# A planned order of instructions, and VectorE operations that use both SBUF ports kept apart from GpSimd in the plan

## Chip, cores, metric

The kernel runs on one core of one Trainium2 chip. Its time is device microseconds (us) of one execution; what is given is the median of several. VectorE is DVE in the profile, ScalarE is ACT, GpSimd is POOL, TensorE is PE (its weight loads PEld), SyncE is SP.

## What is computed

Two sequences of 1024 tokens, 288 features, run through four layers one after the other. Layers L0 and L1 are quantised transformer blocks: self-attention (16 heads of 18), cross-attention to 154 context tokens with a mask, and a feed-forward part of 1152. L2 and L3 are plain cross-attentions with two softmaxes, one over 86 and one over 68 context tokens, whose outputs are added.

```python
def quant_act(x):
    s = max(abs(x), axis=-1) / 127 + 1e-8
    q = clip(round(x / s), -127, 127)
    return q, s, sum(q, axis=-1)
def quant_linear(q, s, qsum, w, b):      # w quantised row by row, with a zero point zw
    acc = q @ qw.T - qsum * zw
    return acc * (s * sw) + b
# L0, L1
h = layer_norm(x, g1, b1); x = x + lin(attn(lin(h), lin(h), lin(h)))
h = layer_norm(x, g2, b2); x = x + lin(attn(lin(h), cond @ wk2.T, cond @ wv2.T, mask))
h = layer_norm(x, g3, b3); x = x + lin(gelu(lin(h)))
# L2, L3
x = x + sdpa(q, k, v) @ Wo.T + sdpa(q, k_vip, v_vip) @ Wo_vip.T
```

Every `lin` of L0 and L1 on the tokens is a `quant_act` followed by a `quant_linear`.

## The kernel before

The tokens stay in SBUF as `x`, 16 chunks of 128 tokens. Self-attention takes a head group of four heads and 512 queries at a time, in two sweeps: one finds the maximum of each row of logits (PE L1000 into PSUM, then DVE `tensor_reduce` L1007), the other computes the logits again with the maximum taken off, the exponential (PE L1060, ACT L1062) and the weighted sum of the values (PE L1074, four matmuls of 32 columns side by side, called strips). Cross-attention of L0 and L1 copies the logits out of PSUM (ACT L1040), adds the mask on GpSimd (L1041) and reduces them from SBUF (DVE L1046); its second sweep adds the mask on DVE (L1146). L2 and L3 reduce from PSUM.

Beside these sweeps run the side chains: layer norms, quantisations, weights.

- `ln_quantise`: DVE statistics (L809, L810), the power on GpSimd (L814), scale and shift on ACT (L822), gain and bias on GpSimd (L830, two `tensor_tensor` of 128x288 for each chunk), then `quantise`.
- `quantise`: DVE maximum (L773), scale (L774), reciprocal (L775), GpSimd parts (L780 to L783), DVE multiply and round (L785, `tensor_scalar` in SBUF), ACT (L789), DVE sums (L799, L800).
- `quantise_rows` for weights: small DVE operations (L627 to L637), two `tensor_scalar` for each third (L640, L643), then GpSimd (L648, L653 to L661, and `three`, L613 to L616).
- `split` and `add_to_x` put `tensor_tensor` on GpSimd (L910, L917, L872). `Features.add` (L1210) scales the outputs of L2 and L3 on DVE.

The program text gives only the dependencies. The order on each engine comes from the kernel's own planner at build time: `Plan` reads all instructions, `duration` gives each a latency and a time for which it holds its engine, `forward` is a list scheduler over the five queues (it keeps, for each engine, the ready instructions by rank and starts the best of them when the engine is free), and `backward` makes the ranks. `arrange` runs `forward` with ranks from `backward` 16 times, keeps the plan whose modelled end is the earliest, and chains the instructions of each engine in that order with dependencies that carry no semaphore:

```python
    for line in orders.values():
        for one, other in zip(line, line[1:]):
            order_behind(tc, insts[other], insts[one])
```

So the plan fixes the sequence on each engine, and nothing of the planned times. On the chip an instruction starts when its engine has reached it and its semaphores allow it. In the plan before, DVE and GpSimd know nothing of each other but data.

Of the kernel before, what the change touches and what calls it, by code (L numbers as in the profile page):

```python
# [113 lines left out]
    return t, t - 42  # L114


def region(arg):

    ap = arg.bass_ap
    tensor, dims, at = ap.tensor, list(ap.ap), ap.offset  # L120
    p0, p1 = 0, 1
    if tensor.space != bass.MemoryType.DRAM:
        row = math.prod(tensor.shape[1:])
        p0, at = divmod(at, row)
        step, count = dims.pop(0)
        p1 = p0 + (count - 1) * max(step // row, 0) + 1
    bits = 1
    for step, count in dims:
        if step and count > 1:
            one, made, left = bits, 1, count  # L130
            bits, shift = 0, 0
            while left:
                if left & 1:
                    bits |= one << shift
                    shift += step * made
                left >>= 1
                if left:
                    one |= one << (step * made)
                    made *= 2
    return tensor, p0, p1, bits << at  # L140


class Plan:


    def __init__(self, insts, ties):
        self.insts, n = insts, len(insts)
        self.after = [{} for _ in insts]
        self.need = [0] * n
        self.engine = [None] * n  # L150
        self.times = [(0.0, 0.0)] * n
        self.claims = [[] for _ in insts]
        self.ends = [[] for _ in insts]
        self.bufs, self.turn, self.tag_of = {}, {}, {}
        self.group, self.strip, self.table = {}, [False] * n, [None] * n
        touched, tiles, opened, closed, lead = {}, {}, {}, None, None
        for at, inst in enumerate(insts):
            k, kind = at, type(inst).__name__
            if kind == "BassTilePoolBoundary":
                if inst.op == "release":  # L160
                    closed = k
                    for t in inst.bass_pool_tiles or ():
                        for j in tiles.get(t.name, ()):
                            self.edge(j, k)
                elif closed is not None:
                    opened[inst.bass_pool_name] = closed
                continue
            if not kind.startswith("Inst") or not len(inst.outs):
                continue
            if kind == "InstMatmult" and inst.tile_size[1] == 32:  # L170
                if lead is None or len(self.group[lead]) == 4:
                    lead, self.group[at] = at, []
                k = lead
                self.group[k].append(at)
                self.strip[k] = True
            if kind == "InstActivation" and inst.func != AF.Identity:
                self.table[k] = inst.func
            self.engine[k] = inst.engine.name
            if k == at:
                self.times[k] = duration(inst) if kind != "InstRegisterMove" else (60.0, 60.0)  # L180
            uses = [(a, False) for a in inst.ins] + [(a, True) for a in inst.outs]
            for arg, writes in uses:
                if not hasattr(arg, "bass_ap"):
                    continue
                tensor = arg.bass_ap.tensor
                name, in_dram = tensor.name, tensor.space == bass.MemoryType.DRAM
                if hasattr(tensor, "tag"):
                    if name not in tiles and not in_dram:
                        self.claim(k, tensor)
                        pool = tensor.tag.rsplit("_", 2)[-2]  # L190
                        if pool in opened:
                            self.edge(opened[pool], k)
                    users = tiles.setdefault(name, [])
                    for j in users[:1]:
                        self.edge(j, k, False) if j != k else None
                    users.append(k)
                elif in_dram:
                    continue
                _, p0, p1, bits = region(arg)
                log, kept = touched.setdefault(name, []), []  # L200
                for j, wrote, q0, q1, c in log:
                    if (writes or wrote) and j != k:
                        if p0 < q1 and q0 < p1 and bits & c:
                            self.edge(j, k)
                        elif self.engine[j] == self.engine[k] and wrote and writes:
                            self.edge(j, k, False)
                    if not (writes and p0 <= q0 and q1 <= p1 and j != k and not c & ~bits):
                        kept.append((j, wrote, q0, q1, c))
                kept.append((k, writes, p0, p1, bits))
                touched[name] = kept  # L210
        place = {inst.name: k for k, inst in enumerate(insts)}
        for one, other in ties:
            if self.engine[place[one]] is not None and self.engine[place[other]] is not None:
                self.edge(place[other], place[one], False)
        self.left = {}
        for name, users in tiles.items():
            users = set(users)
            self.left[name] = len(users)
            for j in users:
                self.ends[j].append(name)  # L220
# [20 lines left out]
    def forward(self, rank):  # L241
# [7 lines left out]
        turn, parked = dict.fromkeys(self.bufs, 0), {tag: set() for tag in self.bufs}  # L249
        wakes, clock, busy, window = [0.0], 1.0, 0.0, 0  # L250
        strips, table, last = False, AF.Exp, 0.0
        self.starts, self.took, over = {}, {}, {}

        def blocked(k):
# [48 lines left out]
        while wakes:  # L303
            now = heapq.heappop(wakes)
            moved = True
            while moved:
                moved = False
                for e in free:
                    if free[e] > now:
                        continue  # L310
                    while later[e] and later[e][0][0] <= now:
                        t, r, k = heapq.heappop(later[e])
                        heapq.heappush(now_ready[e], (r, k))
                    while now_ready[e]:
                        r, k = heapq.heappop(now_ready[e])
                        tag = blocked(k)
                        if tag is None and all(
                            slots[g][0][0] + RECLAIM[e] <= now for g, _ in self.claims[k]
                        ):
                            break  # L320
                        offer(k)
                    else:
                        continue
                    start = now
                    lat, held = self.times[k]
                    if e == "PE":
                        while window < int(start / WINDOW):
                            clock = (0.5 if busy < 0.38 else 1.0) if clock == 1.0 else (
                                1.0 if busy >= 0.84 else 0.5
                            )  # L330
                            busy, window = 0.0, window + 1
                        if self.strip[k] != strips:
                            strips = not strips
                            start = max(start, free[e] + (INTO_STRIPS if strips else OUT_OF_STRIPS))
                        busy += (lat - 163) / clock / WINDOW
                        lat, held = (lat - 163) / clock + 163, held / clock
                    elif self.table[k] not in (None, table):
                        table = self.table[k]
                        start = max(start, free[e] + TABLE)
                    self.starts[k] = start  # L340
                    free[e] = start + held
                    heapq.heappush(wakes, free[e])
                    last = max(last, start + lat)
                    orders[e].extend(self.group.get(k, (k,)))
                    for tag, _ in self.claims[k]:
                        self.took[k, tag] = heapq.heappop(slots[tag])[1]
                        turn[tag] += 1
                    finish(k, start, start + lat)
                    for tag, _ in self.claims[k]:
                        retry(tag)  # L350
                    moved = True
# [1803 lines left out]
```

## Time and profile before

| | |
|---|---|
| median of 3 runs | 2097.8 us (2094.75 to 2104.53) |
| profiled execution | 2103.69 us, span 2101.8 us |
| TensorE clock granted, mean | 0.925 |
| busy: PE, DVE, ACT, POOL | 1786.2, 1761.7, 1462.3, 978.1 us |
| chain that ended last | PE 37%, DVE 35%, ACT 11%, DMA 6%, POOL 6%, issue 3% |

The chain is followed back from the last instruction: at each step to what released it, or to the instruction ahead of it on its engine. A group of instructions shows its line, its count, its busy time and the mean of one. The duration of an instruction in the trace includes whatever holds it up once it has begun.

### The profile page before, as it was taken

The numbers are of one execution on the slowest core, as the hardware profiler recorded it, in microseconds if no ns is written. First come the engines' busy times: TensorE is split into PE (matmuls) and PEld (weight loads), VectorE is DVE, ScalarE is ACT, GpSimd is POOL, SyncE is SP. The second block draws the span as 40 slices with busy tenths as digits, with TensorE's granted clock in tenths as the row PEclk, the third lists the DMA queues.
The fourth block names the chain that finished last, engine by engine and source line by source line (L and its number), as shares of the span: only waits on it lengthen the run. The fifth ranks groups of instructions, "written<-read, shape, count | busy, mean of one in ns | idle before, by whom it ended". The sixth has DMA issues, their size and how long they took to land.

```text
span 2101.8 us, 33611 instructions
## 1 busy us (share of the span) xinstructions
PE 1786.2 (85%) x10524; PEld 802.9 (38%) x10524; DVE 1761.7 (84%) x4213; ACT 1462.3 (70%) x2897; POOL 978.1 (47%) x2038
## 2 busy tenths in 40 slices
PE   1689998888788888988978789988888988879998
PEld 1333333433244333333432343333444444444544
DVE  6899999888999797999997988998357797856777
ACT  4268766877578878877877568868676676645554
POOL 4344322655433656544453556534259665413320
PEclk9589999999889999999999889999889999889999
DMA  3533212321100323210024122100033321212331
GB/s 88 162 97 105 80 54 62 87 70 46 41 10 1 116 82 104 63 50 19 16 69 130 43 73 78 55 17 15 23 100 115 98 65 40 59 38 86 97 93 47
DMA packets 160003, 141.58 MB, mean 67 GB/s; under 512 B 44123, under 2 KB 156339, under 8 KB 159760
## 3 DMA queue, kind: packets, MB, share of 16 engines
q1 hardware_dynamic: 154800, 126.63, 21.4%
q0 software_dynamic: 3584, 12.04, 2.3%
q8 instruction: 84, 1.38, 0.3%
q10 hardware_dynamic: 1440, 0.75, 0.1%
q14 instruction: 95, 0.78, 0.1%
HBM read 96.60 MB, written 39.37 MB: 65 GB/s over the span
## 4 chain that ended last, share of the span: by engine, by line
PE 37%; DVE 35%; ACT 11%; DMA 6%; POOL 6%; issue 3%; SPq 1%; ACTq 0%; POOLq 0%; DVEq 0%
DVE L_xattn_amxh L1007 13%; PE L_xattn_aato L1074 5%; PE L_xattn_aats L1060 5%; PE L_xattn_o L1895 4%; PE L_xattn_amx L1000 3%; ACT L_xattn_aatse L1062 3%; PE L_xattn_q L856 2%; DVE L_xattn_batse L1146 2%; PE L_xattn_ato L1074 2%; PE L_xattn_ats L1060 2%; PE L_xattn_co L1761 2%; DVE L_xattn_bmxn L1046 1%; PE L_xattn_cf L856 1%; DVE L_xattn_cqs L773 1%; DVE L_xattn_mxn L1046 1%
## 5 line engine op out<-in xcount | busy, mean ns | idle before, releaser
L1007 DVE TENSOR_REDUCE L_xattn_amxh<-L_xattn_amx 128x1 f32<-128x512 f32 x1024 | 662.6, 679 | 31.5 <-PE L_xattn_amx L1000 30.0
L1062 ACT ACTIVATE L_xattn_aatse<-L_xattn_aats 128x512 f32<-128x512 f32 x1024 | 572.8, 596 | 162.3 <-PE L_xattn_aats L1060 155.4
L1060 PE MATMUL L_xattn_aats<-L_xattn_aqT,kT 120*128 120x512 bf16 x1024 | 374.3, 398 | 52.5 <-ACT L_xattn_aatse L1062 31.3
L1000 PE MATMUL L_xattn_amx<-kT,L_xattn_aqT 108*128 108x512 bf16 x1024 | 368.7, 397 | 49.3 <-DVE L_xattn_amxh L1007 35.1
L1074 PE MATMUL L_xattn_aato<-L_xattn_aatse,L_xattn_av 128*32 128x512 f32 x2048 | 285.7, 629 | 16.4 <-ACT L_xattn_aatse L1062 14.4
L1041 POOL TENSOR_TENSOR L_xattn_bmxm<-L_xattn_bmxm,L_xattn_bm 128x308 f32<-128x308 f32 x256 | 200.2, 788 | 144.9 <-ACT L_xattn_bmxm L1040 138.4
L1062 ACT ACTIVATE L_xattn_atse<-L_xattn_ats 86x512 f32<-86x512 f32 (+1 forms) x256 | 144.1, 590 | 64.2 <-PE L_xattn_ats L1060 59.7
L1060 PEld LDWEIGHTS <-kT 120*128 120x128 bf16 x1024 | 96.3, 100 | 230.2 <-issue 188.2
L1000 PEld LDWEIGHTS <-L_xattn_aqT 108*128 108x128 bf16 x1024 | 99.4, 101 | 177.5 <-issue 121.7
L1046 DVE TENSOR_REDUCE L_xattn_mxn<-L_xattn_mx 128x2 f32<-128x172 f32 (+1 forms) x512 | 130.0, 304 | 11.5 <-PE L_xattn_mx L1030 10.8
L1040 ACT COPY L_xattn_bmxm<-L_xattn_bmx 128x308 f32<-128x308 f32 x256 | 103.7, 416 | 38.2 <-PE L_xattn_bmx L1030 18.8
L1046 DVE TENSOR_REDUCE L_xattn_bmxn<-L_xattn_bmxm 128x2 f32<-128x308 f32 x256 | 116.3, 462 | 12.8 <-POOL L_xattn_bmxm L1041 12.0
L1147 ACT ACTIVATE L_xattn_batse<-L_xattn_batse 128x512 f32<-128x512 f32 x160 | 100.5, 631 | 32.7 <-DVE L_xattn_batse L1146 31.4
L1146 DVE TENSOR_TENSOR L_xattn_batse<-L_xattn_bats,L_xattn_bmT 128x512 f32<-128x512 f32 x160 | 107.4, 682 | 18.7 <-PE L_xattn_bats L1152 8.8
L1060 PE MATMUL L_xattn_ats<-L_xattn_qT,L_xattn_kT 120*86 120x512 bf16 (+1 forms) x256 | 93.8, 401 | 21.3 <-ACT L_xattn_atse L1062 10.1
L1895 PE MATMUL L_xattn_o<-wo,L_xattn_p 128*128 128x288 f32 x320 | 94.0, 425 | 2.5 <-DVE L_xattn_p L1219 2.5
L1074 PEld LDWEIGHTS L_xattn_aato<-L_xattn_aatse,L_xattn_av 128*32 128x32 f32 x2048 | 41.9, 110 | 133.2 <-ACT L_xattn_aatse L1062 78.0
L1030 PE MATMUL L_xattn_bmx<-L_xattn_bkT,L_xattn_bqT 108*128 108x154 bf16 x512 | 74.4, 235 | 7.0 <-ACT L_xattn_bmxm L1040 2.9
L1030 PE MATMUL L_xattn_mx<-L_xattn_kT,L_xattn_qT 108*128 108x154 bf16 x512 | 71.6, 239 | 9.7 <-DVE L_xattn_mxn L1046 6.2
L1074 PE MATMUL L_xattn_ato<-L_xattn_atse,L_xattn_v 68*32 68x512 f32 (+1 forms) x512 | 71.5, 630 | 3.0 <-ACT L_xattn_atse L1062 1.4
L1030 PEld LDWEIGHTS <-L_xattn_bqT 108*128 108x128 bf16 x512 | 45.0, 100 | 68.4 <-issue 41.9
L856 PE MATMUL L_xattn_q<-L_xattn_xT,L_xattn_Wq 96*108 96x512 f32 x144 | 67.1, 600 | 0.7 <-DVE L_xattn_ch L867 0.3
(632 smaller groups left out, 3751.8 us busy)
## 6 DMA issues: line engine op xcount, KB each, us to landing
kT<-L_xattn_akr SPq DMA_DIRECT2D x192, 72.0 KB
L_xattn_aqT<-L_xattn_aqr SPq DMA_DIRECT2D x192, 72.0 KB
L_xattn_bqT<-L_xattn_bqr SPq DMA_DIRECT2D x192, 72.0 KB
L_xattn_qT<-L_xattn_r SPq DMA_DIRECT2D x192, 72.0 KB
L_xattn_akr<-L_xattn_akst SPq DMA_DIRECT2D x16, 324.0 KB
L_xattn_aqr<-L_xattn_aqst SPq DMA_DIRECT2D x16, 324.0 KB
L_xattn_bqr<-L_xattn_bqst SPq DMA_DIRECT2D x16, 324.0 KB
L_xattn_r<-L_xattn_qst SPq DMA_DIRECT2D x16, 324.0 KB
```

Of the source, the lines that this page charges most:

```text
L856: nc.tensor.matmul(ps, lhsT=lhs(k), rhs=rhs(k), start=(k == 0), stop=(k == 2))
L1000: nc.tensor.matmul(sp, lhsT=qt[:KR, j, c * P : (c + 1) * P], rhs=kt[:KR, j, a * 512 : (a + 1) * 512], start=True, stop=True,)
L1007: nc.vector.tensor_reduce(halves[:, a, c, j, :], sp, AX.X, ALU.max, negate=True)
L1030: nc.tensor.matmul(sp[:, j * T : (j + 1) * T], lhsT=qt[:KR, 2 * a + j, c * P : (c + 1) * P], rhs=kt[:KR, 4 * g + 2 * a + j, 0:T], start=Tr ...
L1040: nc.scalar.copy(lm, of)
L1041: nc.gpsimd.tensor_tensor(lm, lm, mask[:, c : c + 1, 0:T].to_broadcast([P, 2, T]), ALU.add)
L1046: nc.vector.tensor_reduce(nm[:, c, 2 * a : 2 * a + 2, n], of[:, :, k0:k1], AX.X, ALU.max, negate=True,)
L1060: nc.tensor.matmul(sp, lhsT=keys(j), rhs=qt[:KM, j, :], start=True, stop=True)
L1062: nc.scalar.activation(e, sp, AF.Exp)
L1074: made = nc.tensor.matmul(po[32 * i : 32 * i + 32, :], lhsT=lhsT, rhs=rhs, start=start, stop=stop)
L1146: nc.vector.tensor_tensor(e, sp, maskT[:, m, :], ALU.add)
L1895: nc.tensor.matmul(ps, lhsT=t[:, c * P : (c + 1) * P], rhs=wo[:, u0 + u, :], start=(u == 0), stop=(u == len(tiles) - 1),)
```

## The change

A function `both_ports` marks DVE operations of three kinds whose tensor operands all lie in SBUF (single-element operands are left out where there is a larger one). `forward` keeps in `port` until when the last marked DVE operation and the last GpSimd operation hold their engines. A GpSimd instruction is not started in the plan before `port["DVE"]`, and a marked DVE operation not before `port["Pool"]`; it goes back to the instructions that become ready later, and the engine takes another one. DMA issues of GpSimd wait for DVE but do not set `port["Pool"]`. No instruction of the program is added or taken away; the order on the engines is planned anew. Its lines from L117 on lie 12 lower, at the end 26 lower.

```diff
+def both_ports(inst):
+    if inst.engine.name != "DVE" or type(inst).__name__[4:] not in (
+        "TensorTensor", "TensorScalarPtr", "TensorCopy"
+    ):
+        return False
+    args = [a for a in inst.ins if hasattr(a, "bass_ap")]
+    tensors = [a for a in args if elements(a) > 1] or args[:1]
+    return all(a.bass_ap.tensor.space != bass.MemoryType.PSUM for a in tensors)
...
+            self.both[k] = both_ports(inst)
...
+        port = {"DVE": 0.0, "Pool": 0.0}
...
                         r, k = heapq.heappop(now_ready[e])
+                        wait = 0.0
+                        if e == "Pool" and self.times[k][1] > 0:
+                            wait = port["DVE"]
+                        elif self.both[k]:
+                            wait = port["Pool"]
+                        if wait > now:
+                            heapq.heappush(later[e], (wait, r, k))
+                            heapq.heappush(wakes, wait)
+                            continue
                         tag = blocked(k)
...
                     self.starts[k] = start
+                    if self.both[k] or e == "Pool" and lat < 2000:
+                        port[e] = start + held
                     free[e] = start + held
```

More of the change, by code (lines that the diff above doesn't have):

```diff
@@ L155, in __init__ @@
         self.group, self.strip, self.table = {}, [False] * n, [None] * n
+        self.both = [False] * n
         touched, tiles, opened, closed, lead = {}, {}, {}, None, None
```

## The prediction

> **What bounds the kernel now.** I read the busy line of the page first, then the chain that ended last, then the stretches in time, and last the single durations of the operations that the change marks.
>
> ```profile
> PE 1786.2 (85%) x10524; PEld 802.9 (38%) x10524; DVE 1761.7 (84%) x4213; ACT 1462.3 (70%) x2897; POOL 978.1 (47%) x2038
> ...
> PE 37%; DVE 35%; ACT 11%; DMA 6%; POOL 6%; issue 3%; SPq 1%; ACTq 0%; POOLq 0%; DVEq 0%
> ```
>
> PE and DVE are equally full, and the chain goes through them in turn. The view by stretches (us of PE, PEld, DVE, ACT, POOL) shows that they are not full at the same time:
>
> ```profile
> 100.00:1500.00 1400.00, 1216.54 (x7222) 501.89 (x7221) 1263.55 (x2773) 1059.43 (x2103) 669.41 (x1412) 0.94 0.22 60
> 1500.00:2100.00 600.00, 527.40 (x3142) 277.91 (x3140) 425.86 (x1242) 368.15 (x733) 265.48 (x519) 0.92 0.27 75
> ```
>
> Up to 1500 us DVE is busy 1263.55 of 1400 us, 90%; after that PE leads (88%) and DVE has room (71%). A DVE operation that lasts too long costs most in the first stretch.
>
> Do marked operations last too long? By line, with minimum/median/maximum in ns:
>
> ```profile
> L785 DVE TENSOR_SCALAR L_xattn_blh<-L_xattn_blh,L_xattn_blqs x32: 278/365/1547, 373.3 to 1597.0; 128x288 f32<-128x288 f32 x32
> L785 DVE TENSOR_SCALAR L_xattn_ba<-L_xattn_ba,L_xattn_boqs x32: 351/362/895, 490.4 to 1750.5; 128x288 f32<-128x288 f32 x32
> L640 DVE TENSOR_SCALAR L_xattn_wv_0w<-L_xattn_wv_0w,L_xattn_wv_0s x6: 415/418/3452, 56.3 to 564.2; 96x288 f32<-96x288 f32 x6
> L1007 DVE TENSOR_REDUCE L_xattn_amxh<-L_xattn_amx 128x1 f32<-128x512 f32 x1024 | 662.6, 679 | 31.5 <-PE L_xattn_amx L1000 30.0
> ```
>
> The same form takes 418 ns or 3452 ns. The timeline (start, us) of DVE, then of POOL, around the 3452 says why:
>
> ```profile
> 564.23 3.45 DVE L640 TENSOR_SCALAR L_xattn_wv_0w<-L_xattn_wv_0w,L_xattn_wv_0s 96x288 f32<-96x288 f32 x1
> 567.61 0.68 DVE L1007 TENSOR_REDUCE L_xattn_amxh<-L_xattn_amx 128x1 f32<-128x512 f32 x1
> ```
> ```profile
> 564.10 0.27 POOL L615 TENSOR_TENSOR L_xattn_wk1s<-L_xattn_wk1s,L_xattn_wk1sq 108x3 f32<-108x3 f32 x1
> 564.33 0.79 POOL L830 TENSOR_TENSOR L_xattn_clh<-L_xattn_clh,L_xattn_ln 128x288 f32<-128x288 f32 x1
> 565.08 0.20 POOL L616 TENSOR_TENSOR L_xattn_wk1sq<-L_xattn_wk1s,L_xattn_wk1sq 108x3 bf16<-108x3 f32 x1
> 565.24 0.79 POOL L872 TENSOR_TENSOR x<-x,L_xattn_bot 128x288 f32<-128x288 f32 x1
> 565.98 1.53 POOL L830 TENSOR_TENSOR L_xattn_clh<-L_xattn_clh,L_xattn_ln 128x288 f32<-128x288 f32 x2
> ```
>
> GpSimd ran without a gap, and the DVE operation came through only when it paused at 567.5. The reduce behind it is no longer than its mean of 679 ns.
>
> **What the collisions cost.** I went through all DVE records, marked those that `both_ports` marks (1007 of 4213, 352.8 us busy), and took the 10th percentile of each form as its undisturbed time. 130 marked instructions are over it by more than 100 ns, 67.5 us in sum, 0.52 us each (29 of L785, 19 of L1210, 31 of L799 and L800). Unmarked ones show nothing: L1007 takes 679 ns with GpSimd running and 679 without. In the other direction 112 GpSimd instructions lose 33.8 us.
>
> How much of that sets the end? I took the chain's pieces in order and matched them with these records: 157 us of marked DVE operations lie on the chain, 50.2 us of it excess. On GpSimd, of which 119 us lie on the chain (12% of its busy time), 12% of 33.8 is 4 us. So 54 us is the most that parting them can give.
>
> **What the change moves.** Nothing is added: all DVE instructions, DMAs and matmuls are the same in both built programs, only their places differ. Marked operations stand 4.2 places later on DVE on average (the others 1.3 earlier), which at 1761.7 us / 4213 = 0.42 us an instruction is 1.8 us. They are bunched: 477 runs of marked operations in place of 546. Of the 130 that were held up, 99 stand later, 19 earlier, 12 in the same place.
>
> *Gain.* If the planned gaps hold on the chip, the 99 of 130 give 0.76 x 50.2 = 38 us. The plan fixes no times; where GpSimd and DVE are out of step, a moved operation finds GpSimd free only as often as chance has it, 1 - 0.47 = 0.53 of the times: 20 us. Ends 0 and 54; I take the middle of 20 and 38, 29 us. What takes the freed place is DVE work that is there already in the first stretch (L1007, 1024 times), so it counts there; after 1500 us it hides behind PE, and 16 of the 67.5 us lie there.
>
> *Cost 1, DVE reduces.* A run of marked operations holds back the L1007 that frees a PSUM buffer for PE. With the undisturbed durations, stretches of over 2 us between two L1007 go from 69 to 91. The waits:
>
> ```profile
> PE L_xattn_amx L1000 <- DVE L_xattn_amxh L1007: 35.1, 98, 1.4
> PEld L_xattn_aato L1074 <- issue: 48.0, 119, 1.4
> ```
>
> One wait is 35.1/98 = 0.36 us, so 22 more are 8 us; nothing if PE has other matmuls at hand, up to 22 x 1.4 = 31 us by the longest. I take 8, the mean.
>
> *Cost 2, strips.* PE changes 904 times between strips and whole matmuls instead of 880, 12 more entries. By the second row a strip's weights wait 48.0/119 = 0.40 us for issue: 0 to 5 us, taken as 3, since most entries show no gap. Table loads on ACT stay 33.
>
> *Cost 3, GpSimd and its queue.* A GpSimd instruction is planned after a marked DVE one; behind it stand the other GpSimd instructions and its 44 DMA issues, and for it wait ACT, PE and the mask's reduce (L1046 <- L1041, 12.0 us). GpSimd has 53% idle, its longest waits are for DVE and ACT themselves (80.4 us of L613 for L1046), and the chip holds it up in these places already: nothing, at most the 12.0 us of L1046 doubled.
>
> Of GpSimd instructions that only write (87 memsets), the trace has three marked operations that began under L1594 or L1609; they lost 2 to 19 ns. The Trainium skill (SBUF — State Buffer, Who interferes with whom) goes further against the change: a DVE operation with two SBUF inputs contends only with a GpSimd one that reads SBUF, so parting such pairs buys nothing. By it 29 us would be a little less; by the rows too, and I leave the sum as it is.
>
> **Sum.** -29 + 8 + 3 = -18 us, on the profiled execution's 2103.69 us (span 2101.8): 2085.7. That execution is 5.9 us above the median of 2097.8, so the median goes to 2080.
>
> **Rivals.** *A, out of step.* A run differs from the plan by more than the 0.5 us of a collision, and as many new ones arise as old ones go. For it: no wait enforces the gap, and GpSimd runs 60% and more in some stretches. Against it: chains of data tie the two every few us. Gain 0 to 10 against costs of 3 to 11: 2098, within 10.
>
> *B, slower: the side chains become late.* A marked operation that finds GpSimd busy is put back, DVE takes something else, and when that ends GpSimd may have begun its next one. The program has 98 such chains (72 runs of `quantise`, 26 of `quantise_rows`). Each stands 1.8 us later by the order. If the end waits for one in four, that is 24.5 x 1.8 = 44 us, and 44 + 11 - 29 = +26: 2124. It decides from 18/1.8 = 10 chains on. For it: after 1500 us the chain goes through such steps and DMA landings, and DVE has room there, so that a later operation is not paid back. Against it: the chains are planned ahead with room, and 1.8 us is under three reduces.
>
> *C, the lock goes away wholly* and costs are nothing: 2097.8 - 54 = 2044.
>
> **Chances.** The forecast's case, with C as its end, 0.55; A 0.20; B 0.25. A measurement of this kernel can tell about 0.5%, 10.5 us, from no change. Faster by more: 0.49 of the forecast's 0.55 and 0.06 of A, 0.55. Within: 0.06 + 0.10 + 0.02 of B = 0.18. Slower: 0.04 of A and 0.23 of B, 0.27. The range reaches from C (2044) to just short of B's 2124: 2045 to 2120; the forecast's own case is 2044 to 2098.
>
> **What would show it.** Right: maxima of L785, L640, L799 and L800 near their medians, the excess of marked operations under 35 us (from 67.5), DVE's busy time down by 30 us or more at the same 4213 instructions, and L1007's share of the chain up. A: excess near 67 us. B: excess down but DVE idle up, and longer waits for L785, L800 or L640's followers. Wrong altogether: a change in PE's clock of over 0.01, or a DMA that lands late and moves a whole stage.

## The result, and the profile after

The changed kernel takes 2113.11 us (median of 8 runs, 2108.62 to 2125.41); the kernel before, beside it, 2096.93 (8 runs). The ratio is 1.0086, 95% interval 1.0061 to 1.0112: slower by 16 us. The forecast was 17 us faster. The profiled execution (span 2106.6 us) is 4.5 us shorter than this kernel's median, and that of the kernel before was 6.8 us longer than its own, so the two traces show only 4.8 us of the 16 in their spans.

The page after, busy line and chain:

```profile
PE 1792.3 (85%) x10524; PEld 805.0 (38%) x10524; DVE 1737.9 (83%) x4213; ACT 1459.7 (69%) x2897; POOL 965.7 (46%) x2038
...
PE 43%; DVE 26%; ACT 13%; DMA 8%; POOL 5%; issue 4%; SPq 2%; ACTq 0%; DVEq 0%; POOLq 0%
```

DVE does the same 4213 instructions in 23.8 us less. But its idle time went from 2101.8 - 1761.7 = 340 to 2106.6 - 1737.9 = 369 us, and the chain moved off it: DVE 35% to 26%, PE 37% to 43%, ACT 11% to 13%, DMA 6% to 8%. The stretches (PE, PEld, DVE, ACT, POOL):

```profile
100.00:1500.00 1400.00, 1217.72 (x7197) 500.49 (x7196) 1245.35 (x2774) 1056.11 (x2096) 661.62 (x1411) 0.93 0.21 60
1500.00:2100.00 600.00, 528.59 (x3150) 278.78 (x3149) 418.59 (x1242) 369.34 (x741) 262.84 (x519) 0.93 0.27 74
```

1400 us now hold as many DVE instructions (2774 after 2773) with 18 us less busy time. The room that was made was not filled.

The collisions did become fewer. By line (minimum/median/maximum ns; L811 is L785 of before, L666 is L640):

```profile
L811 DVE TENSOR_SCALAR L_xattn_blh<-L_xattn_blh,L_xattn_blqs x32: 278/360/1260, 376.3 to 1603.1; 128x288 f32<-128x288 f32 x32
L811 DVE TENSOR_SCALAR L_xattn_ba<-L_xattn_ba,L_xattn_boqs x32: 354/368/910, 489.0 to 1762.0; 128x288 f32<-128x288 f32 x32
L666 DVE TENSOR_SCALAR L_xattn_wv_0w<-L_xattn_wv_0w,L_xattn_wv_0s x6: 418/420/423, 48.1 to 568.8; 96x288 f32<-96x288 f32 x6
```

The 3452 ns are gone. Over all marked operations the excess (over the undisturbed times of before, instances of more than 100 ns) fell from 67.5 us in 130 to 41.6 us in 79, and GpSimd's from 33.8 to 22.2 us. The timeline at the same place, DVE and then POOL:

```profile
566.33 0.68 DVE L1033 TENSOR_REDUCE L_xattn_amxh<-L_xattn_amx 128x1 f32<-128x512 f32 x1
566.93 0.15 DVE L663 TENSOR_SCALAR L_xattn_wv_0s<-L_xattn_wv_0s 96x3 f32<-96x3 f32 x1
567.00 0.42 DVE L666 TENSOR_SCALAR L_xattn_wv_0w<-L_xattn_wv_0w,L_xattn_wv_0s 96x288 f32<-96x288 f32 x1
```
```profile
564.74 2.30 POOL L898 TENSOR_TENSOR x<-x,L_xattn_bot 128x288 f32<-128x288 f32 x3
567.15 0.31 POOL L679 COPY L_xattn_wv_0s<-L_xattn_wv_0s 96x3 f32<-96x3 f32 x1
```

While GpSimd has its three additions, DVE reduces; L666 comes at 567.00, when GpSimd has just finished, and takes 0.42 us. For this operation the plan's gap held on the chip. (GpSimd's L679 began beside it and took 0.31 us, where most of its kind take 0.18.) So the change takes away a good part of the collisions, and the longer time has another cause.

### The profile page after: what moved, and what is told of

It is laid out like the page before. It is cut to its first block, busy times and chain, and to the rows that moved or that the text cites. A ratio compares the mean times of both kernels' runs of the same rounds, so it can differ in the third digit from the quotient of the medians.

```text
span 2106.6 us, 33616 instructions
## 1 busy us (share of the span) xinstructions
PE 1792.3 (85%) x10524; PEld 805.0 (38%) x10524; DVE 1737.9 (83%) x4213; ACT 1459.7 (69%) x2897; POOL 965.7 (46%) x2038
## 4 chain that ended last, share of the span: by engine, by line
PE 43%; DVE 26%; ACT 13%; DMA 8%; POOL 5%; issue 4%; SPq 2%; ACTq 0%; DVEq 0%; POOLq 0%
DVE L_xattn_amxh L1033 10%; PE L_xattn_aato L1100 7%; PE L_xattn_aats L1086 6%; PE L_xattn_amx L1026 5%; ACT L_xattn_aatse L1088 4%; PE L_xattn_o L1921 4%; PE L_xattn_q L882 2%; DVE L_xattn_batse L1172 2%; PE L_xattn_ato L1100 2%; PE L_xattn_ats L1086 2%; PE L_xattn_co L1787 1%; DVE L_xattn_bmxn L1072 1%; DMA L_xattn_aqT<-L_xattn_amxsr 1%; PE L_xattn_cf L882 1%; SPq L964 1%
## 5 line engine op out<-in xcount | busy, mean ns | idle before, releaser
L1033 DVE TENSOR_REDUCE L_xattn_amxh<-L_xattn_amx 128x1 f32<-128x512 f32 x1024 | 663.0, 681 | 39.6 <-PE L_xattn_amx L1026 37.7
L1026 PE MATMUL L_xattn_amx<-kT,L_xattn_aqT 108*128 108x512 bf16 x1024 | 372.7, 401 | 53.3 <-DVE L_xattn_amxh L1033 41.2
L1067 POOL TENSOR_TENSOR L_xattn_bmxm<-L_xattn_bmxm,L_xattn_bm 128x308 f32<-128x308 f32 x256 | 199.7, 785 | 139.7 <-ACT L_xattn_bmxm L1066 135.2
L1026 PEld LDWEIGHTS <-L_xattn_aqT 108*128 108x128 bf16 x1024 | 101.0, 102 | 185.1 <-issue 124.3
L1072 DVE TENSOR_REDUCE L_xattn_mxn<-L_xattn_mx 128x2 f32<-128x172 f32 (+1 forms) x512 | 128.7, 304 | 14.9 <-PE L_xattn_mx L1056 14.4
L1072 DVE TENSOR_REDUCE L_xattn_bmxn<-L_xattn_bmxm 128x2 f32<-128x308 f32 x256 | 116.9, 465 | 15.6 <-POOL L_xattn_bmxm L1067 15.1
L1100 PEld LDWEIGHTS L_xattn_aato<-L_xattn_aatse,L_xattn_av 128*32 128x32 f32 x2048 | 41.2, 109 | 134.7 <-ACT L_xattn_aatse L1088 92.1
L1787 PE MATMUL L_xattn_co<-L_xattn_wfc2t,L_xattn_cgT 117*128 117x288 bf16 x320 | 61.1, 333 | 11.3 <-ACT L_xattn_cgT L1784 10.7
```

The costliest lines, as they stand in the source:

```text
L1026: nc.tensor.matmul(sp, lhsT=qt[:KR, j, c * P : (c + 1) * P], rhs=kt[:KR, j, a * 512 : (a + 1) * 512], start=True, stop=True,)
L1033: nc.vector.tensor_reduce(halves[:, a, c, j, :], sp, AX.X, ALU.max, negate=True)
L1067: nc.gpsimd.tensor_tensor(lm, lm, mask[:, c : c + 1, 0:T].to_broadcast([P, 2, T]), ALU.add)
L1072: nc.vector.tensor_reduce(nm[:, c, 2 * a : 2 * a + 2, n], of[:, :, k0:k1], AX.X, ALU.max, negate=True,)
L1100: made = nc.tensor.matmul(po[32 * i : 32 * i + 32, :], lhsT=lhsT, rhs=rhs, start=start, stop=stop)
```

## Where the saved time went

The first L1033 of a layer needs keys that a side chain has made: layer norm, `quantise`, `linear_T`, `values`, stores, loads (`prepare`). The four self-attention layers take 8 steps of 32 L1007 each; steps 17 and 25 begin the two layers of L1. From the traces I took when step 16 ended (how far the main sweeps had come), when the last of the side chain's eight `vstage` operations of that layer began, and when step 17 ended; and the same for steps 24 and 25. All in us; the experiments named here follow below.

| kernel | span | step 16 ends | last `vstage` | step 17 ends | step 24 ends | last `vstage` | step 25 ends |
|---|---|---|---|---|---|---|---|
| before | 2101.8 | 704.4 | 725.5 | 756.1 | 1081.0 | 1111.5 | 1147.3 |
| after | 2106.6 | 687.6 | 715.2 | 748.3 | 1084.5 | 1115.1 | 1149.2 |
| e4, collisions charged | 2089.7 | 705.8 | 716.2 | 748.3 | 1091.8 | 1104.1 | 1135.2 |
| e9, put back blindly | 2183.3 | 716.8 | 757.5 | 790.1 | 1128.4 | 1162.7 | 1196.4 |

The `vstage` rows of before, after and e9 for the first of the two layers (first and last start):

```profile
L867 DVE SCALAR_TENSOR_TENSOR vstage<-L_xattn_av,L_xattn_ast,L_xattn_wv_0row x8: 507/513/519, 691.5 to 725.5; 128x288 f32<-128x288 f32 x8
```
```profile
L893 DVE SCALAR_TENSOR_TENSOR vstage<-L_xattn_av,L_xattn_ast,L_xattn_wv_0row x8: 504/510/519, 684.3 to 715.2; 128x288 f32<-128x288 f32 x8
```
```profile
L887 DVE SCALAR_TENSOR_TENSOR vstage<-L_xattn_av,L_xattn_ast,L_xattn_wv_0row x8: 501/506/519, 725.2 to 757.5; 128x288 f32<-128x288 f32 x8
```

In the changed kernel the main sweeps led by 16.8 us at step 16, the side chain by 10.3, and one step later the lead was 7.8. In e4 the sweeps led by nothing, the side chain by 9.3, and step 17 ended at the same 748.3. Step 17 ends 31 to 33 us behind the last `vstage` in all four, step 25 31 to 36 us: these two hand-overs go by the side chain, not by the sweeps. The traces of all 20 kernels of this document bear it out. In them step 17 ends 30 to 36 us and step 25 31 to 37 us behind its `vstage`, and the span goes with the start of the second of these (the correlation, 1 at the most, is 0.97, without e9 0.90) and not with the end of step 16 (0.29, without e9 -0.20). The hand-over at step 9 is not of this kind: in the kernel before, its last `vstage` starts 147 us ahead of the end of that step.

So 9 of the 16.8 us were given back at the first hand-over. By the next layer the changed kernel's side chain had fallen from 10.3 us ahead to 3.6 us behind, and step 25 ended 1.9 us late. The second hand-over itself cost nothing more, since the sweeps had lost 11 us by then, between the ends of steps 17 and 24. PE was busy 5.1 us longer in that stretch (292.65 after 287.56 us, at a granted clock of 0.93 after 0.95) and DVE 3.7 us; what the rest waited for was not taken apart.

Are the side chains late because of the marked operations? One can match the DVE instructions of two kernels one by one and compare their starts. Of those that start between 100 and 400 us in the kernel before, the marked ones start 5.8 us later in the changed kernel on average, and the L1007 0.7 us earlier. Of those between 756 and 1081 us the marked ones start 1.2 us later, and the L1007 4.5 us earlier. So in these stretches the marked operations fell 6.5 and 5.7 us behind the reduces. In e6, e7, e1 and e12, which put them back as well, it is 6 to 10 us; in e3, e5 and e16, which know nothing of ports, -4 to +1 us.

The chain of the changed kernel at the first of the two hand-overs (start, us, what):

```profile
709.17 0.66 PE L_xattn_ak L882 x3
...
710.60 0.52 DVE vstage L893
711.12 0.02 issue
711.13 3.50 DMA L_xattn_avr<-vstage
...
717.01 0.75 DVE L_xattn_aqy L978
...
719.32 3.43 DMA kT<-L_xattn_akr
722.76 0.38 issue
723.14 0.81 PE L_xattn_amx L1026 x3
```

Here the chain goes through the side chain's matmuls, `vstage`, its stores, and the loads of `kT`, and only then do the first L1026 of the new layer start. An L1033 that came 17 us earlier is of no use.

## The experiments

Two theories. *Theory 1:* a marked operation that is put back becomes late, because the plan gives DVE another operation meanwhile; the side chains are late with it, and they set the hand-overs. *Theory 2:* the order of 33,000 instructions is so sensitive that any new plan is some 16 us off, whatever it knows of ports. "Excess" is that of the marked operations, counted as above; "places" is how much later than before they stand on DVE in the built order, on average. Ratios are to the kernel before beside them; they come from the single runs, and so can differ a little from what the medians give.

| run | plan | us | ratio (95%) | excess, us | places |
|---|---|---|---|---|---|
| before | no ports | 2097 to 2099 | 1 | 67.5 | 0 |
| e3 | no ports, 15 passes | 2110.7 | 1.0067 (1.0044 to 1.0089) | 76.7 | -0.1 |
| e5 | no ports, 2 ns | 2100.3 | 1.0012 (0.9998 to 1.0026) | 70.5 | -1.4 |
| e16 | no ports, 40 passes | 2088.1 | 0.9945 (0.9925 to 0.9965) | 64.4 | -0.4 |
| after | put back | 2113.1 | 1.0086 (1.0061 to 1.0112) | 41.6 | 4.2 |
| e6 | put back, 2 ns | 2109.5 | 1.0057 (1.0036 to 1.0079) | 38.7 | 4.8 |
| e7 | put back, 11 passes | 2111.4 | 1.0061 (1.0038 to 1.0084) | 39.7 | 4.0 |
| e12 | put back, GpSimd gives way | 2110.5 | 1.0056 (1.0034 to 1.0079) | 38.8 | 5.4 |
| e1 | only DVE put back | 2120.9 | 1.0121 (1.0102 to 1.0139) | 38.2 | 6.0 |
| e2 | only GpSimd put back | 2107.1 | 1.0052 (1.0039 to 1.0065) | 80.0 | -1.2 |
| e8 | put back once | 2107.3 | 1.0039 (1.0021 to 1.0056) | 51.4 | 3.6 |
| e9 | put back blindly | 2177.9 | 1.0383 (1.0358 to 1.0409) | 72.1 | 7.2 |
| e4 | charged only | 2095.2 | 0.9993 (0.9976 to 1.0010) | 66.7 | 0.5 |
| e11 | charged only, 40 passes | 2092.7 | 0.9965 (0.9947 to 0.9982) | 63.6 | 0.7 |
| e10 | charged, marked ones hurried | 2119.6 | 1.0087 (1.0056 to 1.0118) | 70.3 | -3.7 |
| e13 | put back for one due within 1 us | 2097.5 | 0.9989 (0.9972 to 1.0005) | 62.1 | 1.5 |
| e14 | put back for one due within 4 us | 2094.5 | 0.9976 (0.9961 to 0.9991) | 55.0 | 2.8 |
| e15 | put back for waits over 600 ns | 2074.9 | 0.9890 (0.9872 to 0.9908) | 52.2 | 1.5 |
| e17 | as e15, 2 ns | 2077.6 | 0.9906 (0.9884 to 0.9928) | 54.8 | 2.2 |
| e18 | put back for waits over 400 ns | 2090.4 | 0.9960 (0.9946 to 0.9974) | 43.1 | 2.6 |

### The two halves of the change: e1, e2

```diff
 # e1, against the change
-                        if e == "Pool" and self.times[k][1] > 0:
-                            wait = port["DVE"]
-                        elif self.both[k]:
+                        if self.both[k]:
                             wait = port["Pool"]
 # e2, against the change
                         if e == "Pool" and self.times[k][1] > 0:
                             wait = port["DVE"]
-                        elif self.both[k]:
-                            wait = port["Pool"]
```

> Half of the change: in the plan a marked DVE operation waits for GpSimd, but GpSimd does not wait for it. Theory 1 (marked operations put back make the side chains late, and these set when a layer can end): all of the loss is here, 2106 to 2120 us, and the excess of marked operations stays near the 43 us of the change. Theory 2 (a new plan of this program differs by chance by as much as the 16 us seen, whatever it knows of ports): any time from 2080 to 2120, without relation to the excess.

> The other half: GpSimd waits in the plan for a marked DVE operation, and DVE never waits. Theory 1: no marked operation is put back, so the time stays with the kernel before, 2090 to 2104 us, with the excess of marked operations at 55 to 70 us. Theory 2: any time from 2080 to 2120.

With DVE alone put back the excess is as low as in the change and the time higher than the change's, 2120.9 us, just over what Theory 1 allowed. With GpSimd alone put back nothing is won (excess 80.0), and the time is 2107.1, over its range too. DVE's half brings all of the fewer collisions and also the largest loss; that e2 loses too spoke for Theory 2 as well.

### How much a plan scatters: e3, e5, e16, and e6, e7

```diff
-PASSES = 16
+PASSES = 15     # e3; 40 in e16; 11 in e7, on the change
-HANDOVER = {"PE": 37.0, "Activation": 34.0, "DVE": 34.0, "Pool": 33.0, "SP": 300.0}
+HANDOVER = {"PE": 37.0, "Activation": 34.0, "DVE": 36.0, "Pool": 33.0, "SP": 300.0}   # e5; e6 on the change
```

> The kernel before with 15 in place of 16 passes of the planner, so that another of its plans is kept, with nothing about ports. Theory 1: 2090 to 2104 us, as the kernel before. Theory 2: over 10 us away from 2097, up or down.

> The kernel before with one number of the planner moved by 2 ns (what a DVE result takes to reach its reader, 36 in place of 34), nothing about ports: a third plan without them, beside before (2098) and 15 passes (2111). Theory 2 (plans scatter by chance): another time within 2090 to 2115, and excess of marked operations 60 to 80 us. Theory 1 (only putting back costs): 2092 to 2104.

> The kernel before with 40 passes, nothing about ports: a fourth plan without them and the control of the plan that charges collisions with 40 passes (2093). Theory 1: 2090 to 2111 like the other plans without ports, excess 60 to 80 us. If more passes alone made the gain: 2088 to 2096.

> The same 2 ns in the changed kernel: a second plan that keeps the ports apart. Theory 1: 2106 to 2122, above the mean of the plans without ports. Theory 2: within 2090 to 2120, as likely below as above the mean of the plans without ports (about 2103). Excess of marked operations 35 to 48 us by both.

> The changed kernel with 11 passes in place of 16: a third plan that keeps the ports apart. Theory 1: 2106 to 2125. Theory 2: within 2090 to 2120, as likely below 2103 as above. Excess 35 to 48 us by both.

Four plans that know nothing of ports take 2088 to 2111 us (before, e3, e5, e16; mean 2099). So one plan against one other says nothing certain about 16 us, and Theory 2 holds that far; e3 moves marked operations by 0.1 places on average and costs 13 us, outside the 2090 to 2104 of Theory 1, and e16 lies just below its 2090 to 2111. But the three plans of the change lie at 2109.5, 2111.4 and 2113.1, mean 2111, close to the slowest of the four, and they do so with 26 to 29 us less excess than before. The means differ by 12 us, and that is the best estimate of what belongs to the change, the rest to the plan that was drawn; with a scatter of 23 us in the others, that 12 is itself rough. In the traces of these seven kernels the mean spans differ by 9 us, of which 4 are there when step 25 ends; the rest comes behind it, where no hand-over was taken apart.

### What lateness costs: e9

```diff
 # against the kernel before, with both_ports and self.both of the change
+        put_back = set()
...
                         r, k = heapq.heappop(now_ready[e])
+                        if self.both[k] and k not in put_back:
+                            put_back.add(k)
+                            heapq.heappush(later[e], (now + 100.0, r, k))
+                            heapq.heappush(wakes, now + 100.0)
+                            continue
```

> The kernel before, and each marked DVE operation is put back once by 100 ns when its turn comes, whatever GpSimd does; GpSimd waits for nothing. In the built order they stand 7.2 places later than before (4.2 in the change), with nothing won for it. Theory 1 (putting back makes side chains late): clearly slower than the change, 2115 to 2140, excess of marked operations 55 to 75 us. Theory 2 (chance alone): 2090 to 2115 as the other plans without ports.

2177.9 us, 81 us slower, farther than Theory 1 allowed and far outside all scatter. 100 ns for each of 1007 operations would be 101 us if every one were on the path and nothing else happened; the order shows that something else does: they stand 7.2 places later, 3 us at 0.42 us an instruction. In the table of hand-overs its side chain is 32 us late at the first layer and 51 at the second, and the steps behind it by 34 and 49. DVE has only 11 us more to do (1773.1 us busy). The mean granted clock was 0.915 against 0.925, so a part may be PE's. That putting back alone, with nothing else changed, makes the side chains late and the kernel slow is shown by this. How much of the change's own loss is of this kind, it does not show.

### Charging the collision instead: e4, e11, e10

```diff
 # e4, against the change: nothing is put back
-                        wait = 0.0
...
-                        if wait > now:
...
+                    if e == "Pool" and held > 0:
+                        start = max(start, port["DVE"])
+                    elif self.both[k]:
+                        start = max(start, port["Pool"])
                     self.starts[k] = start
 # e11: PASSES = 40.  e10, against e4:
-            heapq.heappush(later[e], (t, rank[k], k))
+            heapq.heappush(later[e], (t, rank[k] - (2000.0 if self.both[k] else 0.0), k))
```

> The plan charges the collision and puts nothing back: a marked DVE operation that is chosen while GpSimd runs holds DVE until GpSimd is done, and a GpSimd one the same way, as the trace shows it on the chip. Theory 1: no lateness by putting back, 2085 to 2100 us, excess of marked operations 50 to 70 us, DVE busy near the 1762 us of before. Theory 2: any time from 2080 to 2120.

> The plan that only charges collisions, with 40 passes in place of 16, so that another of its plans is kept. Theory 1: as the one with 16 passes, 2088 to 2102. Theory 2: 2090 to 2115. Marked operations within 1 place of before, excess 60 to 75 us.

> The plan that only charges collisions (2095), with the rank of marked operations brought forward by 2 us, so that they stand 3.7 places earlier than in the kernel before. Theory 1: no lateness, 2080 to 2097, at an excess of 60 to 80 us. Theory 2: 2090 to 2115.

A planner that knows of the collision and leaves the order of urgency alone gives 2095.2 and 2092.7 us, within the scatter of plans without ports (e16, with as many passes as e11, has 2088.1), at an unchanged excess. Knowing the price does not help by itself. e10 was a miss of Theory 1: marked operations 3.7 places earlier are no gain but cost 18 us by the ratio and 22 by the medians. So it is not only the lateness of marked operations: bringing this whole class forward, out of the order of the ranks, costs too. Presumably others are late then; its last `vstage` before step 25 starts at 1118.8 us, 7 us later than before, but why was not taken apart, and it is one plan.

### Which lateness: e8, e12, e13, e14

```diff
 # e12, against the change: GpSimd leaves the gap to a waiting DVE operation of higher rank
+                        if e == "Pool" and wanted and min(wanted.values()) < r and self.times[k][1] > 0:
+                            held_back.append((r, k))
+                            continue
                         if wait > now:
+                            if e == "DVE":
+                                wanted[k] = r
...
 # e8, against e4: put back once, then charged
+                        if self.both[k] and k not in put_back and port["Pool"] > now:
+                            put_back.add(k)
...
 # e13, against e4: put back only for an operation that is nearly as urgent (4000.0 in e14)
+                        if self.both[k] and port["Pool"] > now and now_ready[e] and (
+                            now_ready[e][0][0] - r < 1000.0
+                        ):
+                            heapq.heappush(later[e], (port["Pool"], r, k))
+                            heapq.heappush(wakes, port["Pool"])
+                            continue
```

> The change, and in the plan GpSimd does not begin an instruction of lower rank while a marked DVE operation of higher rank waits for it, so that such an operation waits for one GpSimd instruction at most. Its place is still 5.4 later, since DVE takes another operation meanwhile. Theory 1: as the change or slower, 2106 to 2122: it is the other DVE operation that makes it late, not a queue of GpSimd instructions. Theory 2: 2090 to 2120. If the queue on GpSimd were the cause, 2095 to 2104.

> A marked DVE operation that finds GpSimd busy is put back once, to the end of the GpSimd instruction that runs; if it then finds the next one running it is started all the same and the plan charges the wait. Theory 1: less lateness than the change, so between the plan that charges only (2095) and the change (2113), about 2100, with an excess between 42 and 67 us. Theory 2: within 2088 to 2118, without relation to the excess.

> The plan that charges collisions, and a marked DVE operation is put back only if the best other operation that DVE has ready is due less than 1 us later than it by the planner's rank. They stand 1.5 places later than before (4.2 in the change). Theory 1 (the cost is lateness of urgent operations): 2085 to 2100 us, under the change's 2113 clearly, at an excess of marked operations of 45 to 60 us. Theory 2 (chance): 2090 to 2115.

> The same with 4 us in place of 1 us; 2.8 places later. Theory 1: between e13 and the change, 2090 to 2108, at an excess of 40 to 55 us. Theory 2: 2090 to 2115.

With GpSimd giving way the time is the change's, 2110.5: a queue of GpSimd instructions is not what makes them late, which leaves what DVE takes instead. Put back once at most: 2107.3, between. Put back only where nothing urgent waits: 2097.5 and 2094.5, out of the change's range, the second at 2.8 places and 55.0 us of excess (e13's 62.1 us is above the 45 to 60 that Theory 1 expected, and e14 was expected to be the slower of the two). That less urgent lateness costs nothing fits Theory 1; by time alone, both are also within the scatter of plans without ports.

### Putting back only where the wait is long: e15, e17, e18

```diff
 # against e4; 400.0 in e18; e17 has the 2 ns as well
+                        if self.both[k] and port["Pool"] > now + 600.0:
+                            heapq.heappush(later[e], (port["Pool"], r, k))
+                            heapq.heappush(wakes, port["Pool"])
+                            continue
```

> The plan that charges collisions, and a marked DVE operation is put back only if GpSimd will run for more than 600 ns yet, about as long as the reduce that DVE takes meanwhile; 1.5 places later. Theory 1: 2085 to 2100, excess 45 to 60 us. Theory 2: 2090 to 2115.

> The rule of e15 (put back only if GpSimd runs for more than 600 ns yet, else charge) with the 2 ns of e5 and e6, so another plan of the same rule; 2.2 places later. If the rule makes the gain: 2072 to 2092. If e15 was a lucky plan: 2092 to 2112. Excess 45 to 58 us by both.

> The rule of e15 with 400 ns in place of 600: more operations are put back, 2.6 places later. If the rule makes the gain: 2075 to 2097, a little more late than e15. If e15 was a lucky plan: 2092 to 2112. Excess 42 to 55 us by both.

The operation that DVE takes instead is often L1007 with its 680 ns. By this reckoning a marked operation that is put back for a wait of 200 ns is late by three times that, and one that would wait 700 ns loses nothing. Two plans of that rule take 2074.9 and 2077.6 us, 1.1% and 0.9% faster than before and below all four plans without ports; at 400 ns it is 2090.4, with less excess (43.1) and more places (2.6). e15 came out below what either theory had allowed (2085 at the least); e17 and e18 lie where they were expected if the rule makes the gain. The best order of the three thus doesn't have the fewest collisions. That 600 ns is good because a reduce takes 680 stays an argument: only 400 and 600 were tried. The page of e15:

```profile
PE 1777.2 (86%) x10524; PEld 797.1 (39%) x10524; DVE 1751.4 (85%) x4213; ACT 1459.3 (70%) x2897; POOL 979.8 (47%) x2038
...
PE 44%; ACT 19%; DVE 19%; POOL 6%; DMA 6%; issue 4%; SPq 1%; ACTq 0%; POOLq 0%; DVEq 0%
```

DVE is busy 13.5 us longer than in the changed kernel, and the span (2070.3 us) is 36.3 us shorter. And its `vstage` row of the first hand-over, against 725.5 of before and 715.2 of after:

```profile
L892 DVE SCALAR_TENSOR_TENSOR vstage<-L_xattn_av,L_xattn_ast,L_xattn_wv_0row x8: 502/506/518, 675.2 to 705.2; 128x288 f32<-128x288 f32 x8
```

The side chain is 20 us ahead of before here, and step 17 ended at 738.0, 18 us ahead.

## Why the prediction was wrong, point by point

**The excess** of marked operations: predicted under 35 us when right, measured 41.6; 26 us gone, GpSimd's 11.6 besides. DVE's busy time fell by 23.8 us. The 30 us or more that were to show there did not come, and the maxima of L785's rows are still 1260 and 910 ns. The plan's gaps do hold on the chip more often than chance: e9, which moves the operations and parts nothing, has an excess of 72.1 us. But the gain of 29 of the 50.2 us on the chain supposed that 58% go, and 38% of the whole went. The term counted only the 130 that had been held up. Of these, 96 are free in the changed kernel and 50 us went with them, but 45 others are held up now that were not before, with 24 us. Rival A (out of step, excess near 67 us) is refuted, and so is C, since three fifths of the excess are still there.

**The step that failed** is the gain's place. I took the excess that lay on the chain of before as time that comes off the end, because DVE work was there to fill it in the first stretch. It did fill, for eight steps (9 to 16): the sweeps led by 16.8 us. But the chain of before only says what was last in that order. At the two layers of L1 the sweeps wait for a side chain, and in the changed kernel its marked operations fall some 6 us behind the reduces, so the room on DVE stayed empty (idle time up by 29 us) and the lead was 7.8 us after the first of these layers began and gone by the second. I had asked that the share of L1007 in the chain go up; it went from 13% to 10%.

**The term that was missing** is lateness. The sum had 0 for it; it stood only in rival B, as 44 us for one chain in four, with a chance of 0.25. Two of B's signs came, excess down and DVE idle up; the third, longer waits for L785, is not there (ACT's wait for it in `L_xattn_cg` was 10.6 us and is 10.5). B's 1.8 us for each chain came from places alone; in the traces the marked operations fell 5.7 and 6.5 us behind the reduces in two stretches. That one chain in four counts was a guess, and no run counts them. Were the gain and the costs as predicted, 16 + 29 - 11 = 34 us of lateness would be left, two fifths of e9's 81 us, at 4.2 places in place of e9's 7.2; but the gain that reached the end was never measured by itself, so this is a reckoning and not a result.

**The small terms.** PE's waits for the reduce:

```profile
PE L_xattn_amx L1026 <- DVE L_xattn_amxh L1033: 41.2, 95, 2.8
PEld L_xattn_aato L1100 <- issue: 36.1, 96, 0.8
```

35.1 to 41.2 us, 6 where 8 were predicted. That it fits is luck: the 22 more waits did not come (95 after 98), and each is longer, 0.43 after 0.36 us, the longest 2.8 after 1.4. The strips' 3 us did not come: their wait for issue fell from 48.0 to 36.1. GpSimd's term, nothing to 12, shows in the mask's reduce (L1072 for L1067): 15.1 after 12.0 us. PE's clock over the whole span, 0.929 after 0.925, does not explain a longer time.

**What no step considered** is the scatter of plans: 2088 to 2111 us without any knowledge of ports. A forecast from one plan to another could not be surer than that.

**The part on memsets** stays open: no run left them out.

## What to carry to other kernels

- A list scheduler that puts an instruction back for a short wait pays with the whole length of what the engine takes instead. Compare the two before putting back; here putting back only for waits over 600 ns, against a reduce of 680 ns, gained 1%, and putting back always lost 0.6 to 0.9%.
- Time that is freed on a busy engine counts only up to the next place where its work waits for a side chain. Look for these hand-overs, and whether the change moves the side chain or the sweeps.
- Before a small change of a planner is judged, draw a few more plans that differ in nothing of interest, and compare groups of plans.

## What the runs showed of the chip that I had not expected

In the kernel before, L640 with its 3.45 us was held up not by one GpSimd instruction but by a row of them: L615 ended and five more ran through while it waited. GpSimd did not even pause at 567.5, as I had read it; the row behind those that the prediction shows is

```profile
567.47 0.28 POOL L661 COPY L_xattn_wk1sq<-L_xattn_wk1sq 108x3 bf16<-108x3 bf16 x1
```

This case is rare: during 120 of the other 129 held-up operations at most one further GpSimd instruction began, and never more than three. And 100 ns of delay on each of 1007 operations of together 353 us, in the plan alone, cost 81 us on the chip.
